# Two attention steps on one core: queries finished by transfers, gathers, exponentials and stores in a new order

## The chip, the core and the metric

The kernel runs on one core of a Trainium2 chip. A core has five engines that run side by side: PE (matrix multiplication), DVE (vector), ACT (scalar functions), POOL (a second vector engine, which also issues the indexed gathers) and SP (which issues most transfers). Each engine works through its own list of instructions strictly in order, and waits where an instruction needs something that another engine or a transfer has not finished. The metric is the device time of one execution in microseconds (us). Three executions of the kernel before took 1345.72, 1345.82 and 1351.75 us; the median is 1345.82 us.

## The reference

`x` has 3327 rows of 256 numbers, `adj` is a sparse 3327 x 3327 matrix with a full diagonal. One layer computes, in float32:

```python
X = maximum(layernorm(x), 0)
R = (adj + eye) / row sums
Xf = Xa = X;  Z = 0
for n in range(2):                      # two steps
    q = Xa @ W1.T @ W2.T;  k = Xa @ W3.T
    p = softmax(q @ k.T)
    A = p, kept where it belongs to the top 0.9 of its row's mass, renormalised
    Xf = R @ Xf
    Xa = A @ Xa
    Z += Xf @ U1[n].T + Xa @ U2[n].T
out = x + layernorm(X + Z) * ln_g + ln_b
```

The softmax has width 3327; the kernel pads it to 3328 = 26 x 128 columns (one padding column).

## The kernel before, in words

Rows are handled in 26 tiles of 128 (`t` = 0 to 25). The program has a preamble (normalisation, transposes, keys and queries of the first step, products with `U1`), a first step over the 26 tiles, a stretch between the steps, a second step over 26 tiles, and a short end. `guess_graph_layer` is all of it; `search_graph_layer` is a slow fallback that runs only if a proof at the end fails.

For each tile a chain of work runs through the engines:

* `weights`: 16 matmuls of queries and keys (PE), in `CUT` = 4 chunks; after each chunk ACT takes the exponential into a tile `e` of 128 x 3328 and sums it into a column of `za`. The last chunk is written in two instructions (L609, and L611 for the column beside the padding one), so that the padding column keeps the zero that was set once.
* `measured`: estimates the threshold of the top 0.9. In the second step (`measured_twice`) ACT passes three times over the tile (L634, about 3.07 us each), with small column arithmetic between on DVE, ACT and POOL. L677 to L679 on POOL prepare columns for L689 on ACT, which sets the bias of the third pass; L698, L699 and L709 to L713 on POOL, and L703 to L705 on ACT, come after the third pass; L715 on ACT makes the final guess from them.
* `settle`: DVE removes what is above the guess (L730, one pass of two tensor inputs over the whole tile), finds exact candidates with MAX8 instructions, and zeroes everything under the exact threshold (L764, a second such pass).
* `Sums`: PE transposes the tile in seven parts (L810), ACT copies each part out (`eT`, L812), PE multiplies (L824).
* `spread`: R times the features, as six matmuls on rows that an index list picked. The rows are gathered by POOL (L901 and L922, five gathers for each tile); `first_end` (first step) and `finish` (second step: L466, L467, L962, L969 to L972 on POOL, then the store of the output) close a tile.

In iteration `i`, `settle` works on tile `i`, `measured` on tile `i + 1`, and the exponentials on tile `i + 2`. What stands in which order on each engine within one iteration is written by hand: `PLAN[step]` has seven strings, one for each seventh of an iteration, and each letter advances one generator (`d` settle, `m` measured, `n` the rest of the previous `m`, `w` exponentials, `g` gathers, `s` spread, `f` finish, `l` laws, `q` query projection). `OPEN` and `LAST` replace `PLAN` in the first and last iterations of the second step; for iterations 4 to 24 of that step `PLAN[1]` holds. At the end of the program the order of the text is made binding on PE, ACT, DVE and POOL, and on SP up to the second step.

Queries: `wk` holds W3, W1 and W3 side by side, so one product gives keys and first-stage queries; `project` multiplies a tile's queries with W2 (L524, written to both halves of 128 rows), copies the result out (`qT`, L529), and in the first step also makes the columns of statistics (`mq`, `ms`, L526 to L546).

Of the kernel before, what the change touches and what calls it, by code (L numbers as in the profile page):

```python
# [18 lines left out]
P = 128  # L19
N = 3327  # L20
# [325 lines left out]
def guess_graph_layer(ctx, tc, x, adj, w1t, w2t, w3t, u1t, u2t, ln_g, ln_b, out, flag):  # L346
# [44 lines left out]
    w1r = w1t.rearrange("(c p) a -> p c a", p=P)  # L391
# [3 lines left out]
    w2d = const.tile([P, P], F32, tag="w2d", name="w2d")  # L395
    for h in range(2):
        for c in range(2):
            nc.sync.dma_start(w2d[h * DA : (h + 1) * DA, c * DA : (c + 1) * DA], w2t)
    u1 = const.tile([P, ND, 2, D], F32, tag="u1", name="u1")
    u2 = const.tile([P, ND, 2, D], F32, tag="u2", name="u2")  # L400
# [27 lines left out]

    upto = const.tile([P, P], F32, tag="upto", name="upto")
# [21 lines left out]


    w2x = const.tile([P, P], F32, tag="w2x", name="w2x")
# [51 lines left out]
    def moments(step, gram):  # L505
        gs = small.tile([DA, DA + 1], F32, tag="gs", name="gs", bufs=1)
        n = sum(rows_of(t) for t in COUNTED)
        V.tensor_scalar(gs, gram, 1.0 / n, None, ALU.mult)
        pq = ps_t.tile([P, 4, P], F32, tag="pt", name="pq")
        PE.matmul(pq[:, 0, : DA + 1], w2x[:DA, :], gs, start=True, stop=True)  # L510
        V.tensor_copy(qm[:, step, :DA], w2d[:, :DA])
        V.tensor_copy(qm[:, step, DA : DA + 1], pq[:, 0, DA : DA + 1])
        V.tensor_copy(qm[:, step, DA + 1 : 2 * DA + 1], pq[:, 0, :DA])
        V.tensor_scalar(qm[:, step, 2 * DA + 1 :], pq[:, 0, DA : DA + 1], -1.0, None, ALU.mult)


    def project(step, t, queries=True, law=True):

        qp = query_at(t)
        pq = ps_t.tile([P, 4, P], F32, tag="pt", name="pq")  # L520
        pm = pq[:, 1:3, :].rearrange("p a b -> p (a b)")[:, : 2 * DA + 2]
        qT = ms = None
        if queries:
            PE.matmul(pq[:, 0, :], w2d[qp, :], query_of(t), start=True, stop=True)  # L524
        if law:
            PE.matmul(pm, query_of(t), qm[qp, step, :], start=True, stop=True)  # L526
        if queries:
            qT = tpool.tile([P, P], F32, tag="qT", name="qT", bufs=3)
            S.copy(qT, pq[:, 0, :])  # L529
        if not law:  # L530
            return qT, ms
# [15 lines left out]
        return qT, col  # L547
# [35 lines left out]
    def weights(step, t, live, known=True):  # L583

        r = dict(Z=rec[:, step, 3, t : t + 1])
        qT, r["ms"] = yield from project(step, t, law=known and not step)
        if known and step:
            r["ms"] = law_of(t)
        yield
        r["ms"] = r["ms"] or early.get(t)  # L590
        r["e"] = e = es[(2, 3, 0, 1, 4, 5)[t % 6] if step else t % 4]
        r["za"] = za = small.tile([P, CUT + 1], F32, tag="za", name="za")
        live[step, t] = r
        w = HALF * P
        wd = w // CUT
        for n in range(CUT):
            c = n * wd
            pl = ps_l.tile([P, 2, 512], F32, tag="pl", name="pl")
            for a in range(2):
                p = slice(a * DA, (a + 1) * DA)  # L600
                PE.matmul(pl[:, a, :wd], qT[p, :],  # L601
                          keys_of(step, a).rearrange("p a b -> p (a b)")[:, c : c + wd],
                          start=True, stop=True)
            if n < CUT - 1:
                S.activation(e.rearrange("p (a n) -> p a n", a=2)[:, :, c : c + wd], pl[:, :, :wd],  # L605
                             AF.Exp, accum_out=za[:, n : n + 1])
                yield
            else:
                S.activation(e.rearrange("p (a n) -> p a n", a=2)[:, :, c : w - 1], pl[:, :, : wd - 1],  # L609
                             AF.Exp, accum_out=za[:, n : n + 1])  # L610
                S.activation(e[:, w - 1 : w], pl[:, 0, wd - 1 : wd], AF.Exp, accum_out=za[:, n + 1 :])  # L611
# [160 lines left out]
    def prove(step):  # L772
# [6 lines left out]
        for a, c, op in ((tn, 0.0, ALU.is_gt), (t, 0.5 * BIG, ALU.is_lt),  # L779
                         (Z, 1.0e-30, ALU.is_gt), (Z, BIG, ALU.is_lt)):  # L780
            V.scalar_tensor_tensor(ok, a, c, ok, op, ALU.mult)
# [155 lines left out]

    def first_end(t):
        aT = transposed(live.pop(("r", t)))
        yield  # L940
# [8 lines left out]
        nc.sync.dma_start(sx[t], sv)  # L949
# [33 lines left out]
    own_of = {}  # L983
    live, ohs, acs, xgs, done, early = {}, {}, {}, {}, [], {}
    none = iter(())
# [5 lines left out]
    def returned(work):  # L991
        while True:
            try:
                next(work)
            except StopIteration as end:
                return end.value[1]
# [33 lines left out]
    for q in range(HALF + 5):  # L1030
# [31 lines left out]
        if 0 <= q - 1 < HALF:  # L1062
# [7 lines left out]
            turned[k] = pt  # L1070
        if 0 <= q - 4 < HALF and 2 * (q - 4) in COUNTED:
# [3 lines left out]
        if q == 6:  # L1075
            run(begun[0], 1)
        if q in (8, 11, 14):
            run(begun[0], 1)
        if q in (9, 12):
            run(begun[q // 3 - 2], 1)  # L1080
# [3 lines left out]
        if q == 10:  # L1084
            pw = ps_t.tile([P, 4, P], F32, tag="pt", name="pw")
            PE.transpose(pw[:, 0, :], w2d, ident)
            S.copy(w2x, pw[:, 0, :])
    moments(0, pgram[:DA, : DA + 1])
    for k in range(3):
        early[k] = returned(project(0, k, queries=False))  # L1090
# [36 lines left out]
    def refetch(t):  # L1127
# [10 lines left out]
            ("llcmss", "lnms", "lwwnfd", "lcmdsssgggg", "fdsmwqdf", "llmdf", "lmwdg"))  # L1138
# [19 lines left out]
    for step in range(2):  # L1158
        sums = Sums(step, live, xw if step else x0, AHEAD[step])

        for i in range(-1, NT + 2):
# [4 lines left out]
            if step == 1 and i == -1:  # L1166
                run(begun[0])
                prove(0)
                for e in es[4:]:
                    G.memset(e[:, N:NP], 0.0)  # L1170
# [16 lines left out]
            if i >= 0 and valid(i + 3):  # L1187
                later[step, i + 3] = weights(step, i + 3, live)
                work["q"] = itertools.islice(later[step, i + 3], 2 - step)
# [3 lines left out]
            if step == 0 and i >= NT - 3 and i < NT:  # L1193
                work["q"] = itertools.islice(begun[i - NT + 3], 1)
# [30 lines left out]
            for c in ("lcnwqsepb" if i > -1 else "cnwqsepb") if step else "ocmwqseph" + "b" * (i > 0):  # L1225
                run(work[c])
            if step == 0 and i == NT:
                moments(1, gsum)
                for t in range(3):
                    live[1, t]["ms"] = returned(project(1, t, queries=False))  # L1230
# [51 lines left out]
```

## Time and profile before

| | us |
|---|---|
| median of three executions | 1345.82 |
| the profiled execution | 1354.65 |
| its span, first to last instruction | 1352.9 |
| preamble, to the end of the first tile's settle | 108 |
| first step, 25 tiles on (108.2 to 710.6) | 602 |
| between the first step's last tile and the second's first | 81 |
| second step, 25 tiles on (792.0 to 1324.6) | 533 |
| end | 28 |

The boundaries are the starts of L765 (the end of a tile's settle). Over the span PE is busy for 94%, DVE for 86%, ACT for 80%, POOL for 75%. PE's figure counts overlapping matmuls, so it overstates how full PE is. Between two tiles' ends the first step takes 24.1 us on average (260.7 to 622.3, 15 tiles) and the second 21.5 us (L715 from 876.21 to 1284.86, 19 tiles).

### The profile page before, as it was taken

How to read it: one execution, taken by the hardware profiler on the slowest of the kernel's cores; microseconds unless marked ns; L12 is line 12 of the kernel's file. 1: busy time of each engine (PE TensorE's matmuls, PEld its weight loads, DVE VectorE, ACT ScalarE, POOL GpSimd, SP SyncE). 2: the span in 40 equal slices, each digit the busy share in tenths (PEclk: the TensorE clock that was granted, in tenths of full speed). 3: DMA queues.
4: the chain of work that ended last, by engine and by line, in shares of the span. 5: the costliest groups of instructions: out<-in, count | busy, mean ns of one | idle time of the engine just before them, and what ended most of it. 6: DMA issues, size and time to landing. Idle time of an engine off the chain costs nothing.

```text
span 1352.9 us, 22127 instructions
## 1 busy us (share of the span) xinstructions
PE 1269.8 (94%) x6495; PEld 976.5 (72%) x6495; DVE 1164.4 (86%) x3481; ACT 1082.9 (80%) x2368; POOL 1019.6 (75%) x1405
## 2 busy tenths in 40 slices
PE   5989999999999999999999579999999999999985
PEld 4635777878777777777777457777777777777774
DVE  5867799999999999999890689899898989989893
ACT  4385788888888879888763789999998999999951
POOL 5114788888888888887883577888888888888862
PEclk9999999999999999999999879999999999999998
DMA  8634545454454544545443212221212222131200
GB/s 276 205 127 131 146 137 159 125 151 146 136 158 124 160 139 137 157 133 152 125 111 88 73 53 68 74 90 51 91 56 86 64 82 87 54 90 51 91 24 23
DMA packets 92642, 149.77 MB, mean 111 GB/s; under 512 B 15425, under 2 KB 59072, under 8 KB 92512
## 3 DMA queue, kind: packets, MB, share of 16 engines
q1 hardware_dynamic: 75056, 105.37, 24.5%
q0 software_dynamic: 16640, 42.69, 12.4%
q8 instruction: 54, 0.88, 0.3%
q14 instruction: 76, 0.62, 0.1%
q10 hardware_dynamic: 816, 0.20, 0.1%
HBM read 120.93 MB, written 27.28 MB: 110 GB/s over the span
## 4 chain that ended last, share of the span: by engine, by line
DVE 34%; ACT 25%; PE 21%; POOL 11%; issue 5%; DMA 3%; SPq 0%; another core or an unknown queue 0%; DVEq 0%; POOLq 0%; ACTq 0%
ACT ja L634 13%; PE pa L824 8%; DVE cand L735 7%; DVE w L730 5%; DVE e L764 4%; DVE fm L854 4%; PE pl L601 3%; ACT e L605 2%; ACT eT L812 2%; PE pz L1012 2%; PE pt L810 2%; POOL g L713 2%; DVE cand L744 2%; DVE bb L742 2%; POOL xg L922 2%
## 5 line engine op out<-in xcount | busy, mean ns | idle before, releaser
L824 PE MATMUL pa<-xw,eT 128*128 128x256 f32 x1352 | 322.3, 383 | 4.0 <-DVE s L954 4.0
L634 ACT ACTIVATE ja<-e,g 128x3328 uint8<-128x3328 f32 x106 | 325.7, 3072 | 0.1
L824 PE MATMUL pa<-x,eT 128*128 128x256 f32 x1352 | 322.1, 379 | 0.0
L824 PEld LDWEIGHTS pa<-xw,eT 128*128 128x128 f32 x1352 | 249.9, 190 | 52.7 <-issue 13.8
L824 PEld LDWEIGHTS pa<-x,eT 128*128 128x128 f32 x1352 | 242.8, 190 | 25.8 <-ACT xa L833 0.2
L735 DVE MAX8 cand<-w 128x8 f32<-128x168 f32 (+1 forms) x1040 | 253.4, 319 | 0.0
L901 POOL DMA_INDIRECT ac<-in_adj,index x130 | 202.9, 1561 | 60.2 <-issue 24.4
L812 ACT COPY eT<-pt 128x512 f32<-128x512 f32 (+1 forms) x364 | 199.6, 556 | 43.3 <-PE pt L810 38.7
L922 POOL DMA_INDIRECT xg<-bx,index x130 | 177.2, 1363 | 50.1 <-issue 23.1
L810 PE MATMUL pt<-ident,e 128*128 128x128 f32 x1144 | 176.2, 276 | 18.0 <-DVE e L761 8.6
L810 PEld LDWEIGHTS pt<-ident,e 128*128 128x128 f32 x1144 | 139.7, 144 | 60.1 <-issue 23.6
L730 DVE SCALAR_TENSOR_TENSOR w<-e,g 128x3328 f32<-128x3328 f32 x44 | 166.9, 3793 | 6.4 <-ACT g L715 6.3
L922 POOL DMA_INDIRECT xg<-vx,index x130 | 140.2, 1078 | 34.0 <-issue 29.8
L930 PE MATMUL pr<-xg,ac 128*128 128x257 f32 (+1 forms) x520 | 140.6, 394 | 9.0 <-DVE s L1120 7.3
L764 DVE SCALAR_TENSOR_TENSOR e<-e,rec 128x3328 f32<-128x3328 f32 x40 | 147.2, 3681 | 0.6
L605 ACT ACTIVATE e<-pl 128x832 f32<-128x832 f32 x132 | 113.1, 861 | 31.6 <-PE pl L601 20.7
L930 PEld LDWEIGHTS pr<-xg,ac 128*128 128x128 f32 x520 | 93.7, 194 | 34.5 <-issue 14.0
L601 PE MATMUL pl<-both,qT 64*128 64x416 f32 x416 | 91.8, 539 | 8.3 <-DVE e L1018 3.6
L601 PE MATMUL pl<-after,qT 64*128 64x416 f32 x416 | 95.3, 552 | 1.1 <-ACT e L605 1.1
L854 DVE TENSOR_REDUCE fm<-at 128x4 f32<-128x512 f32 (+1 forms) x133 | 84.5, 635 | 7.0 <-DMA at<-in_adj 5.6
L742 DVE MAX8 bb<-cand 128x8 f32<-128x160 f32 x234 | 75.6, 323 | 4.6
L634 ACT ACTIVATE ja<-x,g 128x3328 uint8<-128x3328 f32 x24 | 73.7, 3072 | 0.0
(260 smaller groups left out, 2132.3 us busy)
## 6 DMA issues: line engine op xcount, KB each, us to landing
at<-in_adj SPq DMA_DIRECT2D x114, 256.0 KB
cx<-ac SPq DMA_DIRECT2D x26, 384.0 KB
ac<-cx SPq DMA_DIRECT2D x26, 384.0 KB
wide<-in_adj SPq DMA_DIRECT2D x8, 832.0 KB
e<-in_adj SPq DMA_DIRECT2D x6, 832.0 KB
own<-bx SPq DMA_DIRECT2D x26, 128.5 KB
x<-in_x SPq DMA_DIRECT2D x13, 256.0 KB
xr<-in_x SPq DMA_DIRECT2D x26, 128.0 KB
```

The source lines that it names most:

```text
L601: PE.matmul(pl[:, a, :wd], qT[p, :], keys_of(step, a).rearrange("p a b -> p (a b)")[:, c : c + wd], start=True, stop=True)
L605: S.activation(e.rearrange("p (a n) -> p a n", a=2)[:, :, c : c + wd], pl[:, :, :wd], AF.Exp, accum_out=za[:, n : n + 1])
L634: S.activation(ja, e, f, bias=guess, scale=sign, accum_out=total)
L730: V.scalar_tensor_tensor(w, e, col(16), e, ALU.is_lt, ALU.mult, accum_out=d2)
L735: V.max(cand[:, 8 * s : 8 * s + 8], w[:, s * SEG : min(NP, (s + 1) * SEG)])
L764: V.scalar_tensor_tensor(e, e, at(1), e, ALU.is_ge, ALU.mult, accum_out=ra)
L810: PE.transpose(pt[:, j, :], e[:, (j0 + j) * P : (j0 + j + 1) * P], ident)
L812: S.copy(eT[:, :w, :], pt[:, :w, :])
L824: PE.matmul(self.pa, eT[:, c - 4 * k, :], self.xa[:, j, :], start=c == 0, stop=c == NT - 1)
L901: G.indirect_dma_start(out=ac[:, k, :], out_offset=None, in_=rows, in_offset=bass.IndirectOffsetOnAxis(ap=index[:, t, k : k + 1], axis=0), ...
L922: G.indirect_dma_start(out=xg[:, k, :w], out_offset=None, in_=rows, in_offset=bass.IndirectOffsetOnAxis(ap=index[:, t, k : k + 1], axis=0))
L930: PE.matmul(pr[:, :w], ac[:, k, :], own if k == KT - 1 else xg[:, k, :w], start=k == 0, stop=k == KT - 1)
```

## The change

1. W1 and W2 are multiplied once, in the preamble (two transposes, two products, two copies), and `wk` holds the product. So `both` holds finished queries; `project` is gone. `asked` copies a tile's queries into the two halves of `qT` by two transfers of 64 x 128 on SP, issued at the head of iteration `i` for tile `i + 3`. `law_once` keeps the statistics, between the first and second chunk of exponentials in the first step. The matrices `w2d` and `w2x` are gone; identities written once take their places.
2. In the second step the last chunk of exponentials is one instruction over all columns, padding included; exp(0) = 1 in the padding column is summed out by a constant -1 in `zas`, and POOL sets the column to zero afterwards (a new MEMSET for each tile, L611 of the changed kernel).
3. The store of `sx` in the first step is issued one tile later (`stores`).
4. `PLAN[1]`: the third and fourth `w` stand ahead of the `m` beside them; the five `g` of an iteration stand together at its end, with the third of the four `f` behind them.

```diff
-    for k, src in enumerate((w3r, w1r, w3r)):
-        nc.scalar.dma_start(wk[:, :, k * DA : (k + 1) * DA], src)
-    w2d = ...
+    nc.scalar.dma_start(w1n, w1t.rearrange("(c p) a -> p c a", p=P))
+    nc.scalar.dma_start(w2n, w2t)
+    for k in (0, 2):
+        nc.scalar.dma_start(wk[:, :, k * DA : (k + 1) * DA], w3r)
...
+    zas = const.tile([P, 4, CUT + 1], F32, tag="zas", name="zas")
+    G.memset(zas[:, :, CUT:], -1.0)
...
-    def project(step, t, queries=True, law=True):
-        qp = query_at(t)
+    def asked(t):
+        qT = tpool.tile([P, P], F32, tag="qT", name="qT", bufs=3)
+        for rows in (low, high):
+            nc.sync.dma_start(qT[rows], query_of(t))
+        return qT
+
+    def law_once(step, t):
         pq = ps_t.tile([P, 4, P], F32, tag="pt", name="pq")
         pm = pq[:, 1:3, :].rearrange("p a b -> p (a b)")[:, : 2 * DA + 2]
-        if queries:
-            PE.matmul(pq[:, 0, :], w2d[qp, :], query_of(t), start=True, stop=True)
-        if law:
-            PE.matmul(pm, query_of(t), qm[qp, step, :], start=True, stop=True)
-        if queries:
-            qT = tpool.tile([P, P], F32, tag="qT", name="qT", bufs=3)
-            S.copy(qT, pq[:, 0, :])
+        PE.matmul(pm, query_of(t), qm[query_at(t), step, :], start=True, stop=True)
...
             if n < CUT - 1:
                 S.activation(e...[:, :, c : c + wd], pl[:, :, :wd], AF.Exp, accum_out=za[:, n : n + 1])
+                if known and not step and n < 2:
+                    r["ms"] = returned(lawful) if n else next(lawful)
                 yield
+            elif step:
+                S.activation(e...[:, :, c : c + wd], pl[:, :, :wd], AF.Exp, accum_out=za[:, n : n + 1])
+                G.memset(e[:, N:NP], 0.0)
             else:
                 S.activation(e...[:, :, c : w - 1], pl[:, :, : wd - 1], AF.Exp, accum_out=za[:, n : n + 1])
                 S.activation(e[:, w - 1 : w], pl[:, 0, wd - 1 : wd], AF.Exp, accum_out=za[:, n + 1 :])
...
+    def stores():
+        while kept:
+            t, sv = kept.popitem()
+            nc.sync.dma_start(sx[t], sv)
+
     def first_end(t):
         aT = transposed(live.pop(("r", t)))
+        stores()
...
-        nc.sync.dma_start(sx[t], sv)
+        kept[t] = sv
...
+        if q == 1:
+            pw = ps_t.tile([P, 4, P], F32, tag="pt", name="pw")
+            for c in range(ND):
+                PE.transpose(pw[:DA, c, :], w1n[:, c, :], ident)
+            V.tensor_copy(w1m, pw[:DA, :ND, :])
+            for c in range(ND):
+                PE.matmul(pw[:, 2 + c, :DA], w1m[:, c, :], w2n, start=True, stop=True)
+            V.tensor_copy(wk[:, :, DA : 2 * DA], pw[:, 2:, :DA])
...
-            ("llcmss", "lnms", "lwwnfd", "lcmdsssgggg", "fdsmwqdf", "llmdf", "lmwdg"))
+            ("llcmss", "lnms", "lwwnfd", "lcmdsss", "fdswmqdf", "llmd", "lwmdgggggf"))
```

The change moves all line numbers by four to twelve. The next fences show three places of the second step, in the middle of it, before and after; names in them are those of the code.

The first place is POOL around L713, whose result L715 on ACT waits for. Before:

```order
L711 TENSOR_TENSOR g<-g 128x1
L712 TENSOR_SCALAR g<-g 128x1
L713 TENSOR_TENSOR g<-g 128x1
L922 DMA xg<-vx,index 128x256
L677 TENSOR_SCALAR g<-g,law 128x1
L678 TENSOR_SCALAR g<-g 128x1
L679 TENSOR_SCALAR g<-g,law 128x1
L969 TENSOR_SCALAR s_12049<-s_12049,rstd,nm 128x256
L970 TENSOR_TENSOR s_12049<-s_12049,gam 128x256
L971 TENSOR_TENSOR xr<-xr,bet 128x256
L972 TENSOR_TENSOR s_12049<-s_12049,xr 128x256
L922 DMA xg<-vx,index 128x256 x4
```

In this order one gather stands between L713 and L677, and four more behind `finish`. The same stretch of POOL now:

```order
L715 TENSOR_TENSOR g<-g 128x1
L716 TENSOR_SCALAR g<-g 128x1
L717 TENSOR_TENSOR g<-g 128x1
L926 DMA xg<-vx,index 128x256 x5
L470 TENSOR_SCALAR rstd<-mv 128x1
L471 TENSOR_TENSOR rstd<-rstd,half 128x1
L972 TENSOR_SCALAR nm<-mv,rstd 128x1
L681 TENSOR_SCALAR g<-g,law 128x1
L682 TENSOR_SCALAR g<-g 128x1
L683 TENSOR_SCALAR g<-g,law 128x1
L979 TENSOR_SCALAR s_12012<-s_12012,rstd,nm 128x256
```

L713 is now L717, L922 is L926, and L677 to L679 are L681 to L683. All five gathers and three small instructions of `finish` stand between L717 and L681.

The second place is POOL a little earlier, before the chain that begins with L698. Before:

```order
L692 TENSOR_SCALAR g<-rec,g 128x1
L693 TENSOR_SCALAR g<-g 128x1
L466 TENSOR_SCALAR rstd<-mv 128x1
L467 TENSOR_TENSOR rstd<-rstd,half 128x1
L962 TENSOR_SCALAR nm<-mv,rstd 128x1
L698 TENSOR_SCALAR g<-oa 128x1
L699 TENSOR_SCALAR g<-rec,g 128x1
```

In this order three instructions of `finish` stand ahead of L698. The same stretch of POOL now:

```order
L696 TENSOR_SCALAR g<-rec,g 128x1
L697 TENSOR_SCALAR g<-g 128x1
L611 MEMSET x_95 128x1
L702 TENSOR_SCALAR g<-oa 128x1
L703 TENSOR_SCALAR g<-rec,g 128x1
```

The three instructions of `finish` have left, and the new MEMSET of the padding column, which needs the last chunk of exponentials, stands ahead of L702 (L698 before).

The third place is ACT from the logarithm that follows the second pass over the tile to the last chunk of exponentials. Before:

```order
L688 ACTIVATE g<-g,one 128x1
L689 ACTIVATE g<-g 128x1
L605 ACTIVATE e_99,za<-pl 128x2x416
L529 COPY qT<-pq 128x128
L812 COPY eT<-pt 128x512
L634 ACTIVATE ja,oa<-e_102,g 128x3328
L812 COPY eT<-pt 128x512
L703 ACTIVATE g<-g,one 128x1
L704 ACTIVATE g<-g 128x1
L705 ACTIVATE g<-g,one 128x1
L609 ACTIVATE e_99,za<-pl 128x2x415
L611 ACTIVATE e_99,za<-pl 128x1
```

In this order both chunks of exponentials (L605, L609) follow the logarithms beside them. The same stretch of ACT now:

```order
L603 ACTIVATE e_99,zas<-pl 128x2x416
L692 ACTIVATE g<-g,one 128x1
L693 ACTIVATE g<-g 128x1
L816 COPY eT<-pt 128x512
L638 ACTIVATE ja,oa<-e_102,g 128x3328
L816 COPY eT<-pt 128x512
L609 ACTIVATE e_99,zas<-pl 128x2x416
L707 ACTIVATE g<-g,one 128x1
L708 ACTIVATE g<-g 128x1
L709 ACTIVATE g<-g,one 128x1
```

The chunks (now L603 and L609) stand ahead of the logarithms (now L692 and L707 to L709), and the copy of `qT` and the single column L611 are gone.

More of the change, by code (lines that the diff above doesn't have):

```diff
@@ L450, in guess_graph_layer @@
     G.memset(bb[:, 0:1], 0.0)
-    w2x = const.tile([P, P], F32, tag="w2x", name="w2x")
+    twice = const.tile([DA, P], F32, tag="twice", name="twice")
+    for rows in (low, high):
+        G.tensor_copy(twice[:, rows], ident[:DA, :DA])
+        for step in range(2):
+            G.tensor_copy(qm[rows, step, :DA], ident[rows, rows])
     def spread_of(rows):
@@ L585, in weights @@
         r = dict(Z=rec[:, step, 3, t : t + 1])
[L586 to L588 removed]
+        qT = asked(t)
         yield
[L590 removed]
+        r["ms"] = law_of(t) if known and step else early.get(t)
+        lawful = law_once(step, t) if known and not step else none
         r["e"] = e = es[(2, 3, 0, 1, 4, 5)[t % 6] if step else t % 4]
[L592 removed]
+        r["za"] = za = zas[:, t % 4, :] if step else small.tile([P, CUT + 1], F32, tag="za", name="za")
         live[step, t] = r
```

53 lines of the change are left out of this document (21 added, 32 removed).

## The prediction

> **What bounds the kernel now.** I first cut the span into stages (start:end, length, busy time of PE, its weight loads, DVE, ACT and POOL, then granted clock and DMA):
>
> ```profile
> 260.70:622.30 361.60, 359.92 (x1912) 283.20 (x1912) 346.02 (x1034) 305.00 (x752) 308.39 (x352) 1.00 0.50 143
> ...
> 876.21:1284.86 408.65, 399.55 (x2057) 312.32 (x2056) 368.06 (x1065) 381.32 (x742) 347.56 (x494) 1.00 0.24 74
> ```
>
> The first row is 15 tiles of the first step (24.1 us each). PE and DVE are both practically full. The second is 19 tiles of the second step (21.51 each): PE and ACT lead, none is full. So there I looked at one instruction after another, first at what L715 on ACT waits for:
>
> ```profile
> L713 POOL TENSOR_TENSOR g<-g x26: 191/192/3685, 770.5 to 1301.6; 128x1 f32<-128x1 f32 x26
> ...
>   ACT g L715: 18.1, 12
> ```
>
> A column of 128 numbers takes 0.19 us, but up to 3.69 in some tiles, and ACT waits for it 12 times. The timelines of POOL, DVE and ACT (start, length) around two tiles show why:
>
> ```profile
> 1131.97 3.65 POOL L713 TENSOR_TENSOR g<-g 128x1 f32<-128x1 f32 x1
> 1135.79 1.12 POOL L922 DMA_INDIRECT xg<-vx,index  x1 [0.17 <-issue]
> 1136.97 3.23 POOL L677 TENSOR_SCALAR g<-g,law 128x1 f32<-128x1 f32 x1
> ...
> 1140.59 0.34 POOL L679 TENSOR_SCALAR g<-g,law 128x1 f32<-128x1 f32 x1
> ...
> 1145.27 0.96 POOL L922 DMA_INDIRECT xg<-vx,index  x1 [0.30 <-issue]
> ...
> 1150.17 0.24 POOL L466 TENSOR_SCALAR rstd<-mv 128x1 f32<-128x1 f32 x1
> ...
> 1151.18 0.26 POOL L962 TENSOR_SCALAR nm<-mv,rstd 128x1 f32<-128x1 f32 x1
> 1151.53 0.26 POOL L698 TENSOR_SCALAR g<-oa 128x1 f32<-128x1 f32 x1
> ...
> 1153.27 0.30 POOL L712 TENSOR_SCALAR g<-g 128x1 f32<-128x1 f32 x1
> 1153.66 0.19 POOL L713 TENSOR_TENSOR g<-g 128x1 f32<-128x1 f32 x1
> ```
>
> ```profile
> 1131.89 3.69 DVE L764 SCALAR_TENSOR_TENSOR x<-x,rec 128x3328 f32<-128x3328 f32 x1
> ...
> 1136.08 3.91 DVE L730 SCALAR_TENSOR_TENSOR w<-x,g 128x3328 f32<-128x3328 f32 x1 [0.29 <-ACT g L715]
> ...
> 1150.92 0.27 DVE L700 TENSOR_SCALAR g<-oa,g 128x1 f32<-128x1 f32 x1 [0.39 <-ACT ja L634]
> ...
> 1153.98 3.69 DVE L764 SCALAR_TENSOR_TENSOR x<-x,rec 128x3328 f32<-128x3328 f32 x1
> ```
>
> ```profile
> 1135.66 0.39 ACT L715 ACTIVATE g<-g 128x1 f32<-128x1 f32 x1 [1.26 <-POOL g L713]
> ...
> 1144.69 0.59 ACT L812 COPY eT<-pt 128x512 f32<-128x512 f32 x1
> 1145.40 0.39 ACT L688 ACTIVATE g<-g,one 128x1 f32<-128x1 f32 x1
> 1145.88 0.39 ACT L689 ACTIVATE g<-g 128x1 f32<-128x1 f32 x1
> ...
> 1147.01 0.25 ACT L529 COPY qT<-pq 128x128 f32<-128x128 f32 x1
> 1147.16 0.60 ACT L812 COPY eT<-pt 128x512 f32<-128x512 f32 x1
> 1147.63 3.09 ACT L634 ACTIVATE ja<-e,g 128x3328 uint8<-128x3328 f32 x1
> ...
> 1150.70 0.59 ACT L812 COPY eT<-pt 128x512 f32<-128x512 f32 x1
> ...
> 1152.43 0.84 ACT L609 ACTIVATE e<-pl 128x830 f32<-128x830 f32 x1
> 1153.18 0.19 ACT L609 ACTIVATION_READ_ACCUMULATOR e<-pl 128x1 f32 x1
> 1153.27 0.15 ACT L611 ACTIVATE e<-pl 128x1 f32<-128x1 f32 x1
> ...
> 1156.35 0.39 ACT L715 ACTIVATE g<-g 128x1 f32<-128x1 f32 x1
> ```
>
> L713 at 1131.97 begins 0.08 after DVE's pass L764 and ends with it: POOL is **held** while a pass of two tensor inputs runs. L677 under L730 fares the same. At 1153.66 L713 comes 0.32 before L764, and nothing waits. From 1135.66 to 1156.35 such a clean tile takes 20.69; tiles with a hold take 22 and more, and the two kinds mostly alternate. The change's question is on which side of L764 the new L717 (L713 before) falls.
>
> **The change part by part, second step.** I count from L715's start (1135.66 is 0).
>
> *ACT.* The copy at 9.03 frees ACT 0.47 later (1147.16 to 1147.63), so the third chunk begins at 9.50 and ends about 10.35. The logarithm's input is there by 9.74, so its wait is gone; L692 comes at 10.35, L693 at 10.83 (0.48 later, as now), and with 0.29 and 0.47 for them and the copy the third pass could begin at 11.59 instead of 11.97. With L611 (0.14) and the second wait gone too, ACT alone would need some 19.9.
>
> *The gathers.* POOL's first gather starts 0.13 after L715, just ahead of L730, and ends at 1.25. The second would start 0.30 later, at 1.55, inside L730, which lasts from 0.42 to 4.33. What a gather does there, the first step shows, on POOL and on DVE:
>
> ```profile
> 504.32 4.38 POOL L922 DMA_INDIRECT xg<-bx,index  x1 [0.16 <-issue]
> ```
>
> ```profile
> 504.18 3.67 DVE L730 SCALAR_TENSOR_TENSOR w<-e,g 128x3328 f32<-128x3328 f32 x1
> ```
>
> It started 0.14 after the pass and ended at 508.70, 0.85 after the pass's end at 507.85. So the second gather ends at 5.18, three more at 0.30 + 0.96 each make 8.96. L470, L471 and L972 take 1.27 (1150.17 to 1151.44), with gaps until 10.3. L681 to L683 need about 0.27 for the first (its row is all hold; L962's is near) and 0.73 from L677's end (1140.20) to L679's (1140.93): **11.4**. L693 needs them, so it runs at 11.46, not 10.83, and the third pass begins at 12.22. Of the 0.38 won, ACT loses 0.63.
>
> The Trainium skill, page SBUF — State Buffer, section Who interferes with whom, says that a DVE instruction with two SBUF inputs takes only the read interface shared with GpSimd, and infers that it leaves descriptor generation alone, which writes. By that the second gather would not be held; the 4.38 us row speaks against it, and the first rival below is this rule's result.
>
> *The guess.* L700 follows the start of the third pass by 3.29, L764 follows L700 by 3.06: so L764 begins 6.35 after the pass. The fourth chunk begins 3.54 after it (1150.70 is 3.07, plus 0.47), and its sum is read at 4.48 (1152.43 to 1153.37 is 0.94). The new MEMSET waits for that; neither it nor its wait has a row in this place. From below it costs 0.1 (the DVE instruction L700 starts 0.1 after the sum it waits for), from above 0.4 (L712's 0.30 added); I take 0.2, near the shortest rows: L702 at 4.7. L712 and L713 follow L698 by 1.74 and 2.13, so L716 comes at 6.4 and L717 at **6.8, 0.5 after L764**. Before, L698 did not wait for the exponentials. L717 is then held in every tile, not in every second, and in the row above 0.08 were enough. L716 is on the edge.
>
> *The tile.* L764 begins at 12.22 + 6.35 = 18.57 and ends at 22.26. L715 started 0.08 after its end (1135.58 to 1135.66): 22.34, or 22.73 if L716 is held too (L713 follows L712 by 0.39). I take the middle, **22.5**, against 21.51: 19 x 1.0 = **+19**. The first iteration with the new table has the hold without the gathers ahead of it: 20.7 becomes about 21.7, **+1**. The four tiles before it keep their table and lose L529 and L611 (0.15 and 0.14): **-1**. PE has 1 us and more to spare in such a tile, so L524's absence pays nothing there.
>
> **First step, and the rest.** What the removed work is worth there stands in the waits and the chain:
>
> ```profile
> DVE fm L854 <- DMA at<-in_adj: 2.7, 4, 1.1
> ...
> DVE fm L854 <- issue: 1.4, 1, 1.4
> ```
>
> ```profile
> SPq L949 <- POOL sv L947: 188.5, 24, 12.4
> ```
>
> ```profile
> 1012.40 0.22 PE pq L524 x2
> ```
>
> PE loses L524, 0.22 a tile (0.31 at most, with the switch behind it). But DVE's list has the same work, and its only waits, 4.1 us in 15 tiles, are for rows of `adj`, which SP asks for late because it stands at the store of `sx` (188 us in all). The later store takes that away. DVE thus gains at most 0.27 a tile, 7 in 25 tiles, and at least nothing, if the two transfers more that SP issues for each tile cost as much: I take **-4**. They have an iteration before they are read; without that cover each tile would wait about as long as L529 took, 0.25.
>
> The preamble now needs the product of W1 and W2 before the first keys:
>
> ```profile
> 11.95 1.18 PE L1069 MATMUL pt<-ident,x 128*128 128x128 f32 x4 [11.95 <-ACT x L1067]
> 13.89 2.07 PE L1056 MATMUL pk<-xw,wk 128*128 128x128 f32 x8 [0.76 <-ACT xw L1052]
> ```
>
> After the transposes at 13.13 come two more (0.6), two copies (0.35 each, as L812's 0.59 is the upper bound), products (0.5 by L1056's eight in 2.07) and three handovers of 0.1: 15.2 instead of 13.89, +1.3. At least nothing, at most 3 (if DVE's list delays the copies). Three L524 leave that stretch, -0.7. I take **+1**. Between the steps the projections of three tiles go: **-1**.
>
> Sum: 19 + 1 - 1 - 4 + 1 - 1 = **+15** on the profiled 1354.65 (span 1352.9 and 1.75 around it), 1370. That execution lies 8.8 above the median, so against the median: **1361**. By its own bounds (22.34 or 22.73 a tile; 0 or -7 in the first step; 0 or +3 at the start) it runs from 1354 to 1371.
>
> **Rivals.** *Gathers pass under L730* (the page's rule as a mechanism of this kernel): five gathers end at 1.25 + 4 x 1.26 = 6.3, L683 at 8.7, before 10.83. L764 then begins at 17.94, and a tile takes 21.7 to 22.1: +0.4 x 19, in all +3: 1349. Against it: 4.38. *L717 slips past L764* by half a microsecond: the first gather then meets L764 and the second L730, each until 0.85 after its end; counted as above, L683 comes 12.6 after the next L715, the third pass at 13.5, and with ACT's 8.3 from there to the next L715 a tile takes 21.8: +5.5, in all about +1: 1347. *Faster: DVE is the late engine.* The passes move together by 0.38, which is DVE's whole wait at L700 (0.39); if DVE falls a further 0.5 behind in every tile, L764 comes after L717, and if the gathers also find gaps between DVE's passes, what is left is PE: the clean 20.69 less 0.31 is 20.4, -1.1 x 19 = -21, and in all -26: 1320. For it: the margin is small, and my MEMSET is a guess. Against it: DVE is busy for only 368 of 409, and the gathers must be lucky too. *The transfers come late:* SP stands at the output's store until POOL has finished a tile, and the queries are behind it; they are asked for more than an iteration ahead, so only a loss of two microseconds a tile (+40, 1385) would show it.
>
> **How the numbers follow.** Forecast 0.54, gathers pass 0.12, L717 slips past 0.10, faster 0.20, transfers late 0.04. About 0.5% (6.7 us) is what a measurement of this kernel can tell from no change. Slower by more: the forecast but for its edge, the late transfers and a little of the first rival, 0.58; within it: the rest of the first two rivals, 0.20; faster: the third and a little of the others, 0.22. The forecast's own range is 1354 to 1371; to leave out no more than 0.2 I go from 1328 to 1372, which holds the milder half of the faster case.
>
> **What would show it.** In the changed profile L717 should last 3.7 us in nearly every tile instead of half of them; the second gather behind it about 3.6; L693 should wait for POOL by some 0.6; L719 should follow L719 by 22.3 to 22.7 without alternation; L707 should no longer wait for DVE. In the first step DVE's waits for `adj` should be gone. I am wrong if L717 ends before L768 begins, if no gather is longer than 1.2 us in the second step, or if tiles there take under 21.5.

## The result, and the profile after

The changed kernel takes 1385.45 us, median of four runs (1379.61 to 1386.31), against 1345.78 us before: a ratio of 1.0283, 95% interval 1.0258 to 1.0308. It is slower by 39.7 us. The forecast was slower by 15, 1361 us, in a range of 1328 to 1372; the sign was right, the size was not. The profiled execution has a span of 1384.1 us, and 1385.8 us as its own time.

The same cut into stages as before, by windows. First the stretch of the first step from the first L734 to the 26th, then 19 tiles of the second step, from one L719 to the one 19 tiles on (length, busy time of PE, its weight loads, DVE, ACT and POOL, granted clock, DMA):

```profile
79.30:688.60 609.30, 602.71 (x3044) 454.05 (x3043) 554.67 (x1689) 498.96 (x1207) 473.21 (x558) 0.99 0.50 143
...
874.32:1311.97 437.65, 406.74 (x2006) 309.45 (x2005) 361.05 (x1062) 376.04 (x684) 335.75 (x514) 0.97 0.24 72
```

The 19 tiles took 408.65 us before and take 437.65 now: 23.03 each instead of 21.51. DVE, ACT and POOL are busy for *less* time in them than before (361 for 368, 376 for 381, 336 for 348). PE alone shows more, 407 for 400 us, with a lower granted clock (0.97 for 1.00). So none of DVE, ACT and POOL has more to do; somebody waits more. The alternation is gone: L719 follows L719 by 23.04 in nearly every tile.

What the engines wait for in the second step, 875 to 1310 us (total, times, longest):

```profile
DVE g L690 <- POOL g L683: 50.5, 19, 4.7
...
ACT g L692 <- DVE g L691: 42.6, 19, 2.9
...
ACT g L719 <- POOL g L717: 2.0, 1, 2.0
```

The wait that the forecast was built on, ACT's for L717, is nearly gone, where it took 13.6 us before. In its place DVE waits 50.5 / 19 = 2.66 us in each tile for L683 on POOL, and ACT 2.24 for what DVE does behind it. The row of L717 itself (shortest, median and longest in ns) agrees: its median is 189 ns.

```profile
L717 POOL TENSOR_TENSOR g<-g x26: 189/189/3642, 767.5 to 1333.0; 128x1 f32<-128x1 f32 x26
```

How L683 became late is told by the chain of waits, from one L719 (1104.59) to the next (1127.65): start, length, and what set the pace ("issue" is time in which the engine waits for nothing that the profile shows):

```profile
1103.98 3.88 POOL xg L926
1107.86 0.30 issue
1108.17 3.31 POOL xg L926
...
1115.32 0.24 POOL rstd L470
...
1117.29 0.35 POOL g L683
...
1117.67 0.22 DVE g L690
...
1118.13 2.32 DVE cand L739 x10
...
1123.29 0.19 DVE g L704
...
1124.84 0.31 POOL g L713
...
1126.27 0.06 POOL g L717
1126.33 0.73 issue
1127.05 3.88 POOL xg L926
```

It closes on itself: 1103.98 to 1127.05 is one tile. Two gathers last 3.88 and 3.31 instead of 0.95; three more, and `finish`, stand between them and L683; L690 waits for L683, and the rest of DVE's list for L690. No run has the five gathers without the hold; as an estimate from these rows, two gathers of 0.95 would bring L683 5.3 us earlier (3.88 + 3.31 - 2 x 0.95). The two passes of DVE that hold the gathers, the waiting instruction, and ACT's third pass behind it:

```profile
1103.17 3.69 DVE L768 SCALAR_TENSOR_TENSOR e<-e,rec 128x3328 f32<-128x3328 f32 x1
...
1106.99 3.67 DVE L734 SCALAR_TENSOR_TENSOR w<-e,g 128x3328 f32<-128x3328 f32 x1
...
1117.67 0.21 DVE L690 TENSOR_SCALAR g<-oa,g 128x1 f32<-128x1 f32 x1 [1.75 <-POOL g L683]
...
1119.40 3.07 ACT L638 ACTIVATE ja<-x,g 128x3328 uint8<-128x3328 f32 x1
...
1126.24 3.69 DVE L768 SCALAR_TENSOR_TENSOR e<-e,rec 128x3328 f32<-128x3328 f32 x1
```

The first gather ends 1.00 after L768's end, the second 0.82 after L734's. Why must L690 wait? It does not read what L683 writes. It *overwrites* column 3 of the guess's tile, which L683 still has to read:

```python
683:  G.tensor_scalar(col(7), col(3), ms(3), ms(8), ALU.mult, ALU.add)
...
690:  V.tensor_scalar(col(3), oa[:, 1:2], float(NP), col(9), ALU.add, ALU.mult)
```

### The profile page after: what moved, and what is told of

Read it like the earlier page. It is cut to its first block, busy times and chain, and to the rows that moved or that the text cites. A ratio compares the mean times of both kernels' runs of the same rounds, so it can differ in the third digit from the quotient of the medians.

```text
span 1384.1 us, 22084 instructions
## 1 busy us (share of the span) xinstructions
PE 1277.3 (92%) x6396; PEld 966.3 (70%) x6396; DVE 1147.5 (83%) x3481; ACT 1070.2 (77%) x2263; POOL 995.2 (72%) x1436
## 4 chain that ended last, share of the span: by engine, by line
PE 53%; POOL 22%; DVE 12%; issue 6%; ACT 5%; DMA 1%; SPq 0%; POOLq 0%; ACTq 0%; DVEq 0%
PE pa L828 23%; POOL xg L926 15%; PE pl L599 7%; PE pt L814 6%; PE pr L934 5%; DVE cand L739 3%; PE pz L953 3%; PE pz L1022 3%; ACT ja L638 2%; DVE cand L748 2%; DVE bb L746 2%; PE pk L1066 1%; POOL rstd L471 1%; PE pk L490 1%; POOL g L713 1%
## 5 line engine op out<-in xcount | busy, mean ns | idle before, releaser
L926 POOL DMA_INDIRECT xg<-vx,index x130 | 225.9, 1738 | 43.2 <-issue 41.0
L905 POOL DMA_INDIRECT ac<-in_adj,index x130 | 188.1, 1447 | 61.5 <-issue 26.9
L926 POOL DMA_INDIRECT xg<-bx,index x130 | 183.4, 1411 | 49.9 <-issue 15.3
L734 DVE SCALAR_TENSOR_TENSOR w<-e,g 128x3328 f32<-128x3328 f32 x44 | 162.6, 3696 | 5.1 <-ACT g L719 4.2
L934 PE MATMUL pr<-xg,ac 128*128 128x257 f32 (+1 forms) x520 | 144.6, 403 | 11.5 <-DVE s L1130 8.5
L768 DVE SCALAR_TENSOR_TENSOR e<-e,rec 128x3328 f32<-128x3328 f32 x40 | 147.3, 3683 | 0.6
L603 ACT ACTIVATE e<-pl 128x832 f32<-128x832 f32 x132 | 114.3, 868 | 35.0 <-PE pl L599 31.6
L599 PE MATMUL pl<-both,qT 64*128 64x416 f32 x416 | 100.3, 547 | 7.7 <-ACT e L603 4.3
L599 PE MATMUL pl<-after,qT 64*128 64x416 f32 x416 | 101.5, 584 | 0.9 <-ACT e L603 0.9
```

The costliest lines, as they stand in the source:

```text
L599: PE.matmul(pl[:, a, :wd], qT[p, :], keys_of(step, a).rearrange("p a b -> p (a b)")[:, c : c + wd], start=True, stop=True)
L734: V.scalar_tensor_tensor(w, e, col(16), e, ALU.is_lt, ALU.mult, accum_out=d2)
L768: V.scalar_tensor_tensor(e, e, at(1), e, ALU.is_ge, ALU.mult, accum_out=ra)
L905: G.indirect_dma_start(out=ac[:, k, :], out_offset=None, in_=rows, in_offset=bass.IndirectOffsetOnAxis(ap=index[:, t, k : k + 1], axis=0), ...
L926: G.indirect_dma_start(out=xg[:, k, :w], out_offset=None, in_=rows, in_offset=bass.IndirectOffsetOnAxis(ap=index[:, t, k : k + 1], axis=0))
L934: PE.matmul(pr[:, :w], ac[:, k, :], own if k == KT - 1 else xg[:, k, :w], start=k == 0, stop=k == KT - 1)
```

## The experiments

**The theories.** A: the order alone costs the time. Five gathers in a row behind L717 meet both passes of DVE, L683 comes late, and the tile waits for it. B: the transferred queries or the padding column cost it. Others are named where they are tested. The intervals are against the kernel before, run beside each.

**The old order in the changed kernel** (`PLAN[1]`; the MEMSET falls behind L717 with it):

```
-("llcmss", "lnms", "lwwnfd", "lcmdsss", "fdswmqdf", "llmd", "lwmdgggggf")
+("llcmss", "lnms", "lwwnfd", "lcmdsssgggg", "fdsmwqdf", "llmdf", "lmwdg")
```

> The changed kernel with the second step's old table of order (four gathers behind `finish`, one behind the guess, as before); all else of the change stays. Theory A (the five gathers in a row are what costs: they hold back L681 to L683 on POOL, and L690 on DVE waits for these): DVE's wait for L683, 2.66 us a tile in the changed kernel, is gone, the tile falls from 23.04 us to 20.7 to 21.5, and the kernel takes 1385 - 19 x 1.5 to 2.3 = 1341 to 1356 us. Theory B (the transferred queries or the padding column cost it): the tile stays above 22.5 and the time above 1375.

Measured: 1344.53 us, ratio 0.9981 (0.9962 to 0.9999). The 19 tiles:

```profile
870.91:1276.09 405.18, 394.56 (x2015) 304.40 (x2014) 366.77 (x1067) 375.34 (x685) 342.81 (x512) 1.00 0.26 77
```

21.33 us a tile, alternating 20.37 and 21.9, and L690 waits no longer for L683. A holds, B falls: all that the change does beside the order comes to a gain of about 3 us here, and its interval reaches almost to nothing.

**The new order alone in the kernel before** (the same two lines the other way round, with matmul queries, L611 on ACT and the early store).

> The kernel before with nothing but the second step's new table of order; queries by matmul, padding by L611 on ACT, and stores stay as they were. Theory A: the gathers are held under L764 and L730, L686 on DVE waits over 2 us a tile for L679, the tile takes 22.5 to 23.0 and the kernel 1368 to 1385 us. Theory B: the order alone costs little, 1340 to 1352 us.

Measured: 1383.41 us, 1.0262 (1.0237 to 1.0287). Its tiles, and DVE's wait at 880 to 1280 us (there L686 and L679 are what L690 and L683 are in the changed kernel):

```profile
873.26:1310.87 437.61, 408.86 (x2061) 313.41 (x2059) 362.16 (x1065) 379.21 (x741) 338.16 (x495) 0.99 0.24 69
```

```profile
DVE g L686 <- POOL g L679: 56.4, 18, 3.3
```

23.03 us, as in the changed kernel. The order alone brings the loss, 1.0262 for 1.0283, with intervals that overlap; A from the other side. With the new order the rest of the change gains nothing that can be told from noise.

**The guess ahead of the gathers.** One new letter writes the next tile's guess before the five gathers, so that L681 to L683 follow L717 directly (the first `m` of the row goes; iteration 4 keeps it, since its guess is not yet begun):

```
-"lwmdgggggf"
+"lwmdxgggggf"   # x: coming[i + 2] = measured(...); next(coming[i + 2])
```

> The changed kernel with one move: the next tile's guess (L625 to L683) is written ahead of the five gathers, so that on POOL L681 to L683 stand between L717 and the first gather; on ACT one copy L816 moves behind the guess. Theory A: the gathers are still held (one or two of them above 3 us), but nobody waits: DVE's wait for L683 is under 0.3 us a tile, the tile takes 20.4 to 21.5, the kernel 1335 to 1356 us. A rival, C (the held gathers cost by themselves, since `finish` and L694 to L697 stand behind them too): the tile stays above 22.3 and the time above 1372.

Measured: 1359.67 us, 1.0083 (1.0059 to 1.0107): 26 us of the loss come back, and L690 waits for ACT only. That is A's main point, and C falls; but 3.7 us lie above A's range, and every tile takes 22.03. The waits at 880 to 1280 us, the row of L717, and POOL and DVE around it say why:

```profile
ACT g L719 <- POOL g L717: 37.3, 18, 2.1
...
L717 POOL TENSOR_TENSOR g<-g x26: 191/3595/3609, 766.1 to 1310.0; 128x1 f32<-128x1 f32 x26
```

```profile
1111.56 3.69 DVE L768 SCALAR_TENSOR_TENSOR e<-e,rec 128x3328 f32<-128x3328 f32 x1
```

```profile
1111.70 3.59 POOL L717 TENSOR_TENSOR g<-g 128x1 f32<-128x1 f32 x1
```

With the wait for L683 gone, L717 starts 0.14 behind L768 in every tile and is held in every tile. This is the mechanism of the forecast: it was there, but hidden behind the larger wait. In the changed kernel the distance is 0.03 (L768 at 1126.24, L717 at 1126.27), and there L717 escapes. The edge lies between 0.03 and the 0.08 of the prediction's row.

**The MEMSET behind L717**, the gathers as in the change (a `yield` before the MEMSET, and a `w` behind `m` in the last row; line numbers from there on are higher by one).

> The changed kernel with the MEMSET of the padding column moved on POOL from ahead of L702 to behind L717; the five gathers stay where they are. Theory A: L717 comes about 0.6 us earlier, but the first gather still starts inside L768 and ends with it, so L683 comes at the same time: 23.0 us a tile, 1380 to 1388 us. Theory D (the MEMSET's wait for the last exponential delays the guess, as the prediction had it): 0.6 us a tile are won, 22.4 us, 1370 to 1376 us.

Measured: 1384.66 us, 1.0275 (1.0256 to 1.0295), 23.0 a tile. POOL and DVE around L718, which is L717 elsewhere:

```profile
893.30 0.19 POOL L718 TENSOR_TENSOR g<-g 128x1 f32<-128x1 f32 x1
...
894.09 4.47 POOL L927 DMA_INDIRECT xg<-vx,index  x1 [0.56 <-issue]
898.86 3.30 POOL L927 DMA_INDIRECT xg<-vx,index  x1 [0.30 <-issue]
```

```profile
893.86 3.68 DVE L769 SCALAR_TENSOR_TENSOR x<-x,rec 128x3328 f32<-128x3328 f32 x1
```

L717 comes 0.56 ahead of the pass instead of 0.03 behind it, and nothing is won: the first gather still starts inside the pass and ends with it. D falls, and the MEMSET is no part of the loss here.

**A column of its own** for L690 and L691, so that nothing is overwritten (the guess's tile grows to 19 columns):

```
-V.tensor_scalar(col(3), oa[:, 1:2], ...);  V.tensor_scalar(col(4), col(3), ...)
+V.tensor_scalar(col(18), oa[:, 1:2], ...); V.tensor_scalar(col(4), col(18), ...)
```

> The changed kernel with one column more in the guess's tile: L690 and L691 on DVE use a column of their own instead of column 3, which L683 on POOL reads before L690 overwrites it. The order of everything stays. Theory A1 (of the loss, the part beyond the late L683 itself is that L690 must not overwrite what L683 has yet to read, so L690, L691 and L692 run behind L683 instead of before it): L690's wait for L683 is gone, L693 now waits for L683, the third pass starts 0.8 to 0.9 us behind L683 instead of 1.77, the tile takes 22.0 to 22.2 us, the kernel 1364 to 1371 us. Rival: another wait holds the pass, the tile stays at 23.0 and the time above 1380.

Measured: 1393.31 us, 1.0353 (1.0320 to 1.0386). The expected 1364 to 1371 was wrong by its sign. The waits moved as A1 said (880 to 1280 us):

```profile
ACT g L719 <- POOL g L717: 36.0, 17, 2.1
ACT g L693 <- POOL g L683: 30.4, 17, 1.8
```

L693 waits for L683, and the third pass starts 0.80 behind L683's end (1123.45 to 1122.65) instead of 1.77. But the tile takes 451.38 / 19 = 23.76. POOL and DVE of one tile:

```profile
1109.92 0.19 POOL L717 TENSOR_TENSOR g<-g 128x1 f32<-128x1 f32 x1
1110.70 4.55 POOL L926 DMA_INDIRECT xg<-vx,index  x1 [0.59 <-PE pt L814]
1115.55 0.95 POOL L926 DMA_INDIRECT xg<-vx,index  x1 [0.30 <-issue]
...
1122.32 0.33 POOL L683 TENSOR_SCALAR g<-g,law 128x1 f32<-128x1 f32 x1
...
1129.90 3.71 POOL L716 TENSOR_SCALAR g<-g 128x1 f32<-128x1 f32 x1
1133.69 0.19 POOL L717 TENSOR_TENSOR g<-g 128x1 f32<-128x1 f32 x1
```

```profile
1129.75 3.69 DVE L768 SCALAR_TENSOR_TENSOR e<-e,rec 128x3328 f32<-128x3328 f32 x1
```

DVE, no longer kept back at L690, starts L768 6.30 behind the third pass instead of 6.84. L716 then starts 0.15 inside L768 and is held for 3.71, and the guess comes behind it. So the wait at L690 had also kept L768 away from the guess: taking it away costs more than it gives. In kind this is the tile that the forecast drew, with L716 held: L693 waits for L683, and the guess is held. The forecast gave it 22.73; it takes 1.03 more, since L683 comes at 12.50 behind L719 instead of 11.4; the rest fits.

**Can a tile be kept clean?** With the old order the clean tiles take 20.37, the held ones 21.9, and a clean one is followed by a held one. ACT's third pass, POOL and DVE ahead of a held L717, in the changed kernel with the old order:

```profile
1139.15 3.08 ACT L638 ACTIVATE ja<-e,g 128x3328 uint8<-128x3328 f32 x1
```

```profile
1143.37 0.26 POOL L972 TENSOR_SCALAR nm<-mv,rstd 128x1 f32<-128x1 f32 x1
1143.71 0.26 POOL L702 TENSOR_SCALAR g<-oa 128x1 f32<-128x1 f32 x1
...
1145.79 3.43 POOL L717 TENSOR_TENSOR g<-g 128x1 f32<-128x1 f32 x1
```

```profile
1145.49 3.69 DVE L768 SCALAR_TENSOR_TENSOR x<-x,rec 128x3328 f32<-128x3328 f32 x1
```

The third pass is over at 1142.23, but L702, which reads its sum, starts 1.48 later: POOL comes to it behind four gathers and L470, L471 and L972. Theory E: POOL's lateness decides on which side of L768 L717 falls. Five kernels move or take away work ahead of L702; all keep the rest of the change.

First `"llmdf", "lmwdg"` to `"llmd", "lmwdgf"`, which puts L470, L471 and L972 behind L717:

> The changed kernel with the old table of order, but L470, L471 and L972 of `finish` moved on POOL from ahead of L702 to behind L717 and the first gather. Theory E (with the old order a tile is held because POOL reaches L702 late, behind four gathers and these three, 1.25 us): L717 falls ahead of L768 in more than half of the tiles; 20.38 us for a clean one; 1330 to 1340 us. Rival: POOL is full anyway and clean and held tiles go on alternating, 1341 to 1348 us.

Measured: 1344.42 us, 0.9994 (0.9976 to 1.0012), alternating 20.38 and 22.1. The rival held.

The same, with L979 on DVE:

```
-G.tensor_scalar(y, y, rstd, nm, ALU.mult, ALU.add)
+V.tensor_scalar(y, y, rstd, nm, ALU.mult, ALU.add)
```

> As the kernel with L470, L471 and L972 behind L717, and L979 (0.55 us on POOL, 128x256) runs on DVE. Theory E: L717 lies 0.5 us or more ahead of L768 in nearly every tile, 20.4 us a tile, 1325 to 1333 us. Rival: DVE becomes late by the 0.3 us that it gains in work, or POOL is full still, and the kernel takes 1338 to 1348 us.

Measured: 1350.47 us, 1.0039 (1.0021 to 1.0057); neither range. No tile but one is held, yet each takes 21.36. On DVE:

```profile
935.44 3.69 DVE L768 SCALAR_TENSOR_TENSOR e<-e,rec 128x3328 f32<-128x3328 f32 x1
...
940.28 0.43 DVE L979 TENSOR_SCALAR s<-s,rstd,nm 128x256 f32<-128x256 f32 x1 [0.95 <-POOL nm L972]
940.63 3.67 DVE L734 SCALAR_TENSOR_TENSOR w<-e,g 128x3328 f32<-128x3328 f32 x1
```

L979 waits between the passes for L972, which POOL reaches late because L470 before it is held by L768. The next two write it behind L772 (`"lwwnfd", "lcmdsssgggg"` becomes `"lwwnd", "lcmdfsssgggg"`), one with `finish` where it was of old, one with it behind L717.

> The changed kernel with the old table of order, and L979 (0.55 us on POOL) on DVE, written a few instructions later there so that DVE does not wait for L972 between L768 and L734. Theory E (POOL's lateness decides on which side of L768 L717 falls): L717, 0.3 us behind L768's start in the held tiles of the kernel with the old order alone, comes about 0.6 us earlier on POOL, so nearly all tiles are clean at 20.4 us and the kernel takes 1326 to 1335 us. Rival: DVE's 0.4 us more or a full POOL keeps the alternation, 1339 to 1347 us.

Measured: 1354.28 us, 1.0070 (1.0045 to 1.0095): neither. L717 starts 0.09 ahead of L768 or 0.02 behind it in every other tile, free; but the gather behind it is caught and lasts to 958.28, L681 is caught by L734, and a tile later L715 is caught, so that a held tile takes 22.8:

```profile
953.52 0.19 POOL L717 TENSOR_TENSOR g<-g 128x1 f32<-128x1 f32 x1
...
953.90 4.38 POOL L926 DMA_INDIRECT xg<-vx,index  x1 [0.16 <-issue]
958.34 2.95 POOL L681 TENSOR_SCALAR g<-g,law 128x1 f32<-128x1 f32 x1
...
974.41 3.65 POOL L715 TENSOR_TENSOR g<-g 128x1 f32<-128x1 f32 x1
```

> As the kernel with L470, L471 and L972 behind L717 and L979 on DVE, whose tiles took 21.36 us without a single held L717 because L979 stood between L768 and L734 on DVE and waited 1.03 us there for L972; now L979 stands behind L772 and four L739. Theory E: that microsecond goes, the tiles stay clean, 20.4 us each, 1328 to 1335 us. Rival: with DVE earlier, L717 (0.57 us ahead of L768 there) falls behind L768 again and tiles alternate, 1340 to 1350 us.

Measured: 1337.15 us, 0.9936 (0.9916 to 0.9957), between both ranges: two tiles in three are clean. Last, the same without L972 (DVE subtracts the mean and multiplies by rstd):

```
-G.tensor_scalar(nm, mv[:, 0:1], rstd, -1.0, ALU.mult, ALU.mult)
-V.tensor_scalar(y, y, rstd, nm, ALU.mult, ALU.add)
+V.tensor_scalar(y, y, mv[:, 0:1], rstd, ALU.subtract, ALU.mult)
```

> As the kernel with L470 and L471 behind L717 and the late L979 on DVE (1337 us, one tile in three held, L717 0.56 and 0.25 ahead and then 0.09 behind the start of L768), without L972 on POOL (0.26 us and a gap of 0.1): the instruction on DVE subtracts the mean and multiplies by rstd instead, which is the same for every tile. Theory E: 0.35 us less on POOL keeps L717 ahead of L768 in all tiles: 20.4 us each, 1326 to 1332 us. Rival: POOL is full, each tile loses another 0.3, and one tile in three or four is still held, 1333 to 1340 us.

Measured: 1333.86 us, 0.9870 (0.9854 to 0.9887). It beats both kernels.

```profile
870.88:1265.02 394.14, 391.07 (x2007) 303.59 (x2006) 370.43 (x1084) 374.79 (x686) 339.51 (x476) 1.00 0.26 80
```

20.74 a tile, PE busy for 391 of 394. The chain of waits runs over PE almost alone from 873 to 1003 us, and for some 86% from 1020 to 1265: the stage is nearly PE's at last. One tile in these 19 is held. The tiles are clean, as E said, but they take 20.37 to 20.74, not 20.4, and the time lies 2 us above E's range and inside the rival's. E is half of the matter: less work ahead of L702 did keep L717 on the right side here, but with as little work three of the five kernels did not gain, two of them because other instructions met a pass (L470 with L979 behind it; the gather, L681 and L715). POOL's lateness alone does not tell the time.

**The kernel before, once more**, for a second profile.

> The kernel before once more, for a second profile. If the 8.8 us between its profiled execution and its median are held tiles, this execution shows another number of them at 1.36 us each, or another pattern; if the alternation is the same in every execution, a difference lies outside the second step's tiles.

Measured: 1346.77 us, against 1354.65 in the first profiled execution. The 19 tiles:

```profile
871.65:1277.23 405.58, 399.51 (x2059) 312.86 (x2058) 369.13 (x1067) 380.92 (x742) 345.50 (x493) 1.00 0.24 74
```

The pattern is another one: every third tile is held, 20.69, 20.69, 22.1, where it was every second. The same program settled into one rhythm in one execution and into another in the other. The stages of several profiled executions side by side, cut at the first and 26th start of L730/L734 and at the first, sixth and 25th of L715/L719 (us):

| | to first L734 | first step | between | 5 tiles | 19 tiles | end |
|---|---|---|---|---|---|---|
| before, first | 81.9 | 611.5 | 77.3 | 105.5 | 408.6 | 68.1 |
| before, second | 77.1 | 612.6 | 77.8 | 104.1 | 405.6 | 67.8 |
| before with the new order | 79.0 | 613.2 | 77.3 | 103.7 | 437.6 | 72.5 |
| changed | 79.3 | 609.3 | 79.2 | 106.6 | 437.7 | 72.1 |
| changed with the old order | 79.9 | 608.0 | 78.2 | 104.9 | 405.2 | 67.2 |

## Why the prediction was right or wrong

**What L693 needs: the step that failed.** "L693 needs them, so it runs at 11.46" took L683's reader for its first dependant. Its first dependant is L690, which overwrites what L683 reads; L691, L692 and L693 run behind that. From L683's end to the third pass the forecast's way takes 0.82 (11.4 to 12.22), and 0.80 where the column is its own; through L690 it is 1.77. Worse, all of DVE's list stands behind L690 for 2.66 us a tile, so DVE became the late engine, and with it the second step of the forecast fell: that L717 is held in every tile.

**The guess.** POOL's side was right: L702 4.7, L716 6.4 and L717 6.8 behind the third pass as forecast, 4.73, 6.47 and 6.87 measured. DVE's side was not: L768 at 6.35 as forecast, 6.84 measured, because of L690. So L717 lies 0.03 behind L768 and is free. With L690's wait taken away L768 is at 6.30, and L716 is held. The forecast called L716 "on the edge"; it was.

**The gathers.** That a gather is held was right, and the rival in which gathers pass under the pass (0.12) falls: 3.88 and 3.31 us here, 4.55 with the column of its own. The Trainium skill, page SBUF — State Buffer, section Who interferes with whom, infers that `tensor_tensor`, a DVE instruction with two SBUF inputs, leaves descriptor generation alone; carried over from `tensor_tensor` to this pass, that does not agree with these rows. But a gather also reads its index list from SBUF, and the new MEMSET, which reads nothing, is not held in any of the eight places in these traces where it falls inside a pass. In the first kernel with L979 late on DVE it starts 0.15 behind L768 (1085.77):

```profile
1085.92 0.10 POOL L611 MEMSET x<- 128x1 f32 x1
```

So it may be the reading that holds a gather; no run separates it from the writing of descriptors.

The forecast let the first gather slip in ahead of L734, as it does behind a held L717. With L717 free it started 0.6 ahead of L719, inside L768, and the second inside L734: L683 came at 13.04 after L719, not 11.4. Between L717 and the first gather POOL waited 0.6 us for nothing that the profile shows. What sets this is open: nearly all free ones have it in the kernels with five gathers in a row behind L717; in the kernel before it is 0.17, behind free and held ones. In the changed kernel the gather would lie inside L768 with 0.17 too. With the column of its own the 0.6 decides: the first gather starts 0.14 inside L734 (1110.56), where 0.17 would have put it 0.28 ahead; four follow it instead of three, and L683 comes at 12.50.

**The rival that came true.** "L717 slips past L764", given 0.10, has the right geometry: the first gather meets one pass, the second the other. Its price was 21.8 a tile. It put L683 at 12.6 (13.04) and the third pass 0.9 behind (1.77 from L683's end); the two make 1.3, and 21.8 + 1.3 = 23.1 is close to the 23.04 measured. One overlooked dependency spoiled the likeliest case and most of the price of the right one. Of the faster rival half came true: it needed DVE 0.5 later, and L768 came at 6.84 for 6.35; the gaps that it needed for the gathers did not come.

**The tile, term by term.** The forecast's 22.34, the lower of its two bounds, is 11.4 to L683, 0.82 to the third pass and 10.12 from there to the next L719. The tile shown above has 13.04, 1.77 and 8.25. L683 and L690 cost 2.6 more than forecast, and the guess that was not held 1.9 less. That the tile lies within 0.6 of the forecast 22.5 is luck, and so in part is the sign: the forecast's loss came mostly from a held guess, the measured one from L683 and L690.

**The sizes, against the first profiled execution.** 19 tiles: +19 forecast, +29.0 measured. The five tiles before these: nothing forecast in sum, +1.1 measured. The end of the step, forecast at nothing: +4.0, nearly all before the last tile's L719, 21.29 us behind the one before it instead of 16.95 (21.14 in the kernel before with the new order). First step: -4 forecast; 608.0 and 609.3 against 611.5 to 613.2 make -3.8 by their means: right. DVE's waits for `adj` are gone there, as forecast. A new one, for the product of the law, is what DVE has instead, behind a PE that is busy for practically the whole window 255 to 616:

```profile
DVE mq L538 <- ACT mq L532: 8.0, 9, 1.7
```

Between the steps: -1 forecast, about +1.2 measured; why is open. The preamble: +1 forecast, 79.3 against 81.9 and 77.1. Two executions of one kernel differ there by more than the term, so it stays open.

**The comparison with the median.** The forecast took the 8.8 us between the first profiled execution and the median as a constant and subtracted it: 1361 instead of 1370. They are no constant. The second profiled execution of the kernel before is shorter by 7.9: 4.8 ahead of the first step, 4.7 from the first L715 on, and 1.6 longer between. The change puts an end to the rhythm: nearly all its tiles are alike, and its profiled execution lies at its median. Against the second execution the spans differ by 1384.1 - 1345.0 = 39.1, near the 39.7 of the medians.

**Of the other signs** named in the prediction: L719 follows L719 without alternation (right, at 23.04 and not 22.3 to 22.7); L707 no longer waits for DVE (right, and of no worth); the second gather lasts about 3.6 (3.31); L693 waits for POOL by 0.6 (wrong: L690 does, by 2.66); L717 lasts 3.7 in nearly every tile (wrong; right, at 3.6, with the guess ahead of the gathers, while with the column of its own it is L716 that is held).

## What to carry to other kernels

When instructions move behind something slow, list for each not only who reads its result but also who overwrites its inputs: that writer, and all that stands behind it on its engine, is late as well. Where long operations on one engine block another, follow each instruction to the side of the edge on which it falls, with the *new* times of both engines; hundredths decide, and a wait that looks like pure loss may be what keeps the two apart. And where a kernel runs in a rhythm of unlike tiles, profile it more than once before an offset is carried over.

## What was not expected of the hardware

The edge is sharp: a POOL instruction that reads a 128x1 column and starts 0.03 after a two-input pass of DVE (128x3328) runs in 0.19 us; one that starts 0.08 or 0.14 after it lasts to its end, 3.65 and 3.59. Near 0.05 both are found: L713 runs free at 806.91 in the kernel before with the new order (L764 at 806.86), and is held for 3.69 at 808.06 in the kernel before (L764 at 808.01). And PE's granted clock was lower where it idled more: 1.00 in the 19 tiles before, 0.97 in those of the changed kernel, where PE is busy for 407 of 438 us. Idle time is not all of it, since the kernel before with the new order shows 0.99 at 409 of 438. It was not the cause here: that kernel has the same tile at 0.99, and the chain of the tile runs over POOL and DVE. But a comparison of PE's busy times across the two kernels has it inside.
